# A decoder layer on one core: GpSimd takes three eighths of attention's products for the first two tiles

## The chip, the cores and the metric

The kernel runs on one core of a Trainium2 chip. The metric is the device time of one execution in microseconds. Three runs of the kernel before gave 707.16, 707.42 and 708.32 us; their median, 707.42 us, is the time before.

## The reference, cut to what matters

A decoder layer with its normalisations behind each part (float32, x of shape 2 x 512 x 1024):

```python
x = layernorm(x + attn(x))            # attention within a token, over the D = 32 channels of 32 heads
x = layernorm(x + xattn(x, ctx))      # fake_quant(x) @ fake_quant(ctx)
x = layernorm(x + ffn(x))             # relu(x@up)**2 @ down + x@fc1@expert@fc2 * routing, normalised

# attn, for each token: q, k, v are [D, H] each; k and v have 8 heads, repeated 4 times
scores = einsum('bsdh,bseh->bsde', q, k) / sqrt(D)
out    = einsum('bsde,bseh->bsdh', softmax(scores), v)
```

The attention mixes the 32 x 32 channel pairs of each token, and no tokens. There is one such small product per token, so it is done elementwise: the tokens lie on the 128 partitions, and the products and sums run along the free dimension.

## The kernel before, in words

The 1024 tokens are eight tiles of 128, t = 0 to 7, and two tiles (`TB = 2`) are a block. The heads that share a k and v are summed first, so each token has q, k and v of 32 x 8 values.

**Front.** TensorE projects tiles 0 and 1 (`project_qk` L153, `project_v` L158) as the weights arrive. Then `fill()` gives it work while the first two tiles go through attention: projections of tiles 2 to 7, then transposes of an expert matrix (L425) and a product of weights (L447). For each tile of `fill()`, x is loaded (`xs`), transposed by TensorE (L134, `pt_x`) and copied from PSUM by ScalarE in two halves (L135, `xT`); the transposes of the next tile stand behind the fifth of the current tile's eight steps. The results are copied by ScalarE (L185, L186) and added by GpSimd's DMAs to biases that lie in DRAM (L191, L192, `qkv_d`); `fetch_qkv` (L175, L176) brings them back when their tile is due. Between these, ScalarE turns the eight tiles of the first context into codes, in three passes each (L364, L367, L370); a context tile's load waits on SyncE's queue for one of the room that earlier ones leave.

**A tile's tokens.** `token_path()` walks through the tiles. `scores(t)` makes q times k in four quarters c (`DC = 8` rows of the 32): a product of 2048 elements for each partition (L463) into `prod`, of which there are two buffers, then a sum over the 8 heads (L469). Both are VectorE's. `exponentials` takes the maximum, subtracts it (L479, on VectorE), and has ScalarE do the exponentials (L482). `attend` sums these (`den`, L488), and makes four more quarters with v: product (L496), sum (L502). Then it multiplies by the reciprocal of `den` (L507) and adds x. For tile 0 that addition (L517) also gives the sum for the mean, and `normalise_aside` does the rest of the normalisation on ScalarE (L335, L340, L342, L348, L349), with an inverse root by GpSimd (L344); tile 1 is normalised on VectorE (`normalise`, L325, its root at L319). `cross` quantises the tile (on ScalarE for tile 0, from L364 on; on VectorE for tile 1, L353 to L355), transposes the codes (`pta`) and multiplies by the context's codes on TensorE (`py`, L654), and normalises again. The sums of the context's codes (`pc`, L580) come in between.

**The feed-forward part.** Block 0 begins when both its tiles are through, at about 144 us of the trace. From then on TensorE works at the feed-forward products (L816, L1046, and for the last two blocks together L931 and L1306), and the attention of tiles 2 to 7 goes on beside it on VectorE. Tile 2's first products stand behind the second normalisation of tile 1 (`last`).

**What sets the order.** The engines run their own queues in order. A planner fixes these when the kernel is built: it takes the instructions as the Python program emits them, with its own costs for each, and may move an instruction ahead of others. `tc.issue_after(x)` pins an instruction behind x on the queue. How far the token path is ahead of the filling work is set by the weights that the generators yield.

Of the kernel before, what the change touches and what calls it, by code (L numbers as in the profile page):

```python
# [12 lines left out]
ALU = mybir.AluOpType  # L13
# [3 lines left out]
P = 128  # L17
# [10 lines left out]
def kernel(  # L28
# [24 lines left out]
    nc = tc.nc  # L53

    B, S, E = x.shape
    _, D, H = wq.shape
    G = wk.shape[2]
# [11 lines left out]
    TB = 2  # L69
# [3 lines left out]
    DC = 8  # L73
# [248 lines left out]
    def normalise(t, name):  # L322

        mean, rstd = mean_rstd([t[:, ts(h, HALF)] for h in range(E // HALF)], name)
        return nc.vector.tensor_scalar(t, t, mean, rstd, ALU.subtract, ALU.mult)  # L325

    def normalise_aside(t, sums, name):

        n = sums.shape[-1]
        parts = small.tile([P, 2], F32, tag="parts", name=f"parts_{name}")  # L330
        minus = parts[:, 0:1]
        if n > 1:
            minus = small.tile([P, 1], F32, tag="minus", name=f"minus_{name}")
        with behind_acted(True):
            nc.scalar.activation(  # L335
                parts[:, 0:n], sums, AF.Copy, scale=-1.0 / E, accum_out=minus if n > 1 else None
            )
        square = attp.tile([P, E], BF16, tag="square", name=f"square_{name}")
        total = small.tile([P, 1], F32, tag="square", name=f"squares_{name}")
        nc.scalar.activation(square, t, AF.Square, bias=minus, accum_out=total)  # L340
        ve = small.tile([P, 1], F32, tag="ve", name=f"ve_{name}")
        nc.scalar.activation(ve, total, AF.Identity, scale=1.0 / E, bias=eps)  # L342
        rstd = small.tile([P, 1], F32, tag="rstd", name=f"rstd_{name}")
        nc.gpsimd.tensor_tensor(rstd, ve, neg_half, ALU.pow)  # L344
        yield 3.0
        shift = small.tile([P, 1], F32, tag="shift", name=f"shift_{name}")
        with behind_acted(True):
            nc.scalar.activation(shift, rstd, AF.Identity, scale=minus)  # L348
        return nc.scalar.activation(t, t, AF.Identity, scale=rstd, bias=shift)  # L349
# [103 lines left out]
            nc.gpsimd.dma_start(e2[ts(l, P), :], row)  # L453


    def scores(t, qk, behind=None):
        q3 = qk[:, 0:DG].rearrange("p (d g) -> p d g", g=G)
        k3 = qk[:, DG : 2 * DG].rearrange("p (e g) -> p e g", g=G)
        s = tokp.tile([P, D, D], F32, tag="s", name=f"s_{t}", bufs=2)
        for c in range(D // DC):  # L460
            prod = tokp.tile([P, DC * D * G], F32, tag="prod", name=f"pqk_{t}_{c}", bufs=2)
            with tc.issue_after(behind.ins) if behind is not None else ExitStack():
                nc.vector.tensor_tensor(  # L463
                    prod.rearrange("p (d e g) -> p d e g", d=DC, g=G),
                    q3[:, ts(c, DC), :].unsqueeze(2).to_broadcast([P, DC, D, G]),
                    k3.unsqueeze(1).to_broadcast([P, DC, D, G]),
                    ALU.mult,
                )
            nc.vector.tensor_reduce(  # L469
                s[:, ts(c, DC), :].rearrange("p d e -> p (d e)"),  # L470
                prod.rearrange("p (c g) -> p c g", g=G), AX.X, ALU.add,
            )
            yield 4.6
        return s
# [11 lines left out]
    def attend(t, xc, s, v):  # L486
        den = small.tile([P, D], F32, tag="den", name=f"den_{t}")
        nc.vector.tensor_reduce(den, s, AX.X, ALU.add)  # L488
        rden = small.tile([P, D], F32, tag="rden", name=f"rden_{t}")
        nc.vector.reciprocal(rden, den)  # L490
        yield 2.0

        o = tokp.tile([P, D, G], F32, tag="o", name=f"o_{t}")
        for c in range(D // DC):
            prod = tokp.tile([P, DC * D * G], F32, tag="prod", name=f"pav_{t}_{c}", bufs=2)
            nc.vector.tensor_tensor(  # L496
                prod.rearrange("p (d g e) -> p d g e", d=DC, g=G),
                s[:, ts(c, DC), :].unsqueeze(2).to_broadcast([P, DC, G, D]),
                v.unsqueeze(1).to_broadcast([P, DC, G, D]),
                ALU.mult,  # L500
            )
            nc.vector.tensor_reduce(  # L502
                o[:, ts(c, DC), :].rearrange("p d g -> p (d g)"),
                prod.rearrange("p (c e) -> p c e", e=D), AX.X, ALU.add,
            )
            yield 4.6
        nc.vector.tensor_tensor(o, o, rden.unsqueeze(2).to_broadcast([P, D, G]), ALU.mult)  # L507

        x3 = xc.rearrange("p (c j) -> p c j", j=J)
        o3 = o.rearrange("p d g -> p (d g)").unsqueeze(2).to_broadcast([P, DG, J])  # L510
        if t == TB - 1:

            nc.vector.tensor_tensor(x3, x3, o3, ALU.add)
            normalise(xc, f"1_{t}")
        else:
            sums = small.tile([P, 1], F32, tag="sum1", name=f"sum1_{t}")
            nc.vector.scalar_tensor_tensor(x3, x3, 1.0, o3, ALU.mult, ALU.add, accum_out=sums)  # L517
            yield 1.0
            yield from normalise_aside(xc, sums, f"1_{t}")
        yield 3.0  # L520
# [151 lines left out]
    def token_path():  # L672
# [5 lines left out]
        def begin(t):  # L678
            xc = xpool.tile([P, E], F32, tag="xc", name=f"xc_{t}")
            nc.sync.dma_start(xc, xf[ts(t, P), :])  # L680
            qk, v = qkv.pop(t)
            if 0 < t < NT - 1:
                fetch_qkv(t + 1)
            at[t] = xc, v, scores(t, qk, last if t == TB else None)
# [13 lines left out]
        for blk in range(NBLK):  # L698
            xcs = []
            x2T = []  # L700
            for i in range(TB):
# [4 lines left out]
                if t == 0:  # L706

                    begin(1)
                    yield next(at[1][2])
                yield from attend(t, xc, done[t], v)  # L710
                if t % (S // P) == 0:
                    b = t // (S // P)
# [763 lines left out]
```

## Time and profile before

| | |
|---|---|
| median of three runs | 707.42 us |
| the profiled execution: its time, and its span from first to last instruction | 707.94 us, 706.2 us |
| granted TensorE clock | 0.991 |
| VectorE products q x k (L463), 32 of them | 72.4 us, 2282 ns each |
| VectorE sums over heads (L469), 32 | 72.3 us, 2277 ns each |
| VectorE products with v (L496), 32 | 72.5 us, 2281 ns each |
| VectorE sums over channels (L502), 32 | 72.0 us, 2265 ns each |
| GpSimd inverse roots (L344), 21 | 21.2 us, 1008 ns each |
| front, 32 to 90 us: busy TensorE, VectorE, ScalarE, GpSimd | 57.70, 54.97, 45.40, 9.62 us |

Busy times are sums over the instructions of an engine in one profiled execution; the mean of one is its own duration, and consecutive independent instructions on VectorE overlap by some 0.08 us, so that a product of 2282 ns comes every 2.20 us. Idle time of an engine costs something only where another waits for it. PE is TensorE's matmuls, DVE VectorE, ACT ScalarE, POOL GpSimd, SP SyncE. L12 is line 12 of the kernel before.

### The profile page before, as it was taken

The page shows a single profiled execution, that of the slowest core. Times are in us where ns is not written, and L with a number is a line of the kernel's source. Part 1 is how long each engine was busy: PE and PEld are TensorE (multiplying, and loading weights), DVE is VectorE, ACT ScalarE, POOL GpSimd, SP SyncE. Part 2 cuts the span into 40 slices and gives each one's busy share as a digit, 9 for nine tenths or more (in the row PEclk, how much of TensorE's full clock was granted, in tenths as well). Part 3 has the DMA queues.
Part 4 walks back from the last instruction along what each step waited for, and adds up shares of the span by engine and source line. Part 5 has one row for each costly group of instructions (what it writes and reads, how often), then busy time and mean ns, then how long its engine had stood idle before and what let it go on. Part 6 is the DMA issues. An engine that isn't in the chain of part 4 may idle for free.

```text
span 706.2 us, 7444 instructions
## 1 busy us (share of the span) xinstructions
PE 682.7 (97%) x2798; PEld 482.6 (68%) x2808; DVE 586.4 (83%) x678; ACT 262.1 (37%) x440; POOL 76.6 (11%) x107
## 2 busy tenths in 40 slices
PE   8999999999999999998999999999999999999991
PEld 3666654578876444477876444478888888888881
DVE  5799987699999999699999960297787688897895
ACT  1297643322636458517626233122251200000252
POOL 1011212200010122001002000020110000001012
PEclk9999999999999999999999999999999999999997
DMA  9989729485446548345536433667997445567733
GB/s 339 304 264 366 204 25 295 104 298 162 144 134 167 184 177 267 136 159 190 173 120 167 176 121 132 233 184 242 355 331 264 153 175 163 171 198 190 208 85 119
DMA packets 70900, 139.08 MB, mean 197 GB/s; under 512 B 5264, under 2 KB 39696, under 8 KB 70864
## 3 DMA queue, kind: packets, MB, share of 16 engines
q1 hardware_dynamic: 60656, 106.87, 44.6%
q0 software_dynamic: 10064, 31.47, 16.1%
q8 instruction: 22, 0.36, 0.2%
q10 hardware_dynamic: 144, 0.26, 0.1%
q14 instruction: 14, 0.11, 0.0%
HBM read 114.99 MB, written 21.50 MB: 193 GB/s over the span
## 4 chain that ended last, share of the span: by engine, by line
PE 40%; issue 6%; DVE 4%; ACT 3%; DMA 2%; POOL 1%; POOLq 0%; DVEq 0%; ACTq 0%
PE pd L1046 9%; PE pp L931 9%; PE ps L1306 5%; PE pp_mm L931 5%; PE pp_tr L931 4%; PE ps_mm L1306 2%; PE ps_tr L1306 2%; PE pu L816 2%; DMA dn<-tw 1%; ACT square L340 1%; PE py L654 1%; DMA y_a<-xc 1%; POOL rstd L344 1%; DVE pav L496 1%; PE pl L816 1%
## 5 line engine op out<-in xcount | busy, mean ns | idle before, releaser
L1046 PE MATMUL pd<-dn,h 128*128 128x512 f32 x320 | 139.3, 593 | 0.0
L816 PE MATMUL pu<-x2T,up 128*128 128x256 f32 x512 | 113.4, 380 | 2.3 <-ACT relu L832 2.3
L1046 PEld LDWEIGHTS pd<-dn,h 128*128 128x128 f32 x320 | 60.3, 190 | 71.8 <-issue 71.3
L816 PEld LDWEIGHTS pu<-x2T,up 128*128 128x128 f32 x512 | 96.4, 190 | 16.9 <-ACT relu L832 3.2
L496 DVE TENSOR_TENSOR pav<-s,v 128x2048 f32<-128x2048 f32 x32 | 72.5, 2281 | 0.0
L463 DVE TENSOR_TENSOR pqk<-qk 128x2048 f32<-128x2048 f32 x32 | 72.4, 2282 | 0.0
L469 DVE TENSOR_REDUCE s<-pqk 128x256 f32<-128x2048 f32 x32 | 72.3, 2277 | 0.1
L502 DVE TENSOR_REDUCE o<-pav 128x64 f32<-128x2048 f32 x32 | 72.0, 2265 | 0.0
L153 PE MATMUL pqk<-wqkv,xT 128*128 128x512 f32 x128 | 65.1, 609 | 1.9 <-DVE wqkv L244 1.6
L158 PEld LDWEIGHTS pv<-wqkv,xT 128*128 128x128 f32 x128 | 24.3, 190 | 24.2 <-issue 22.7
L344 POOL TENSOR_TENSOR rstd<-ve,neg_half 128x1 f32<-128x1 f32 x21 | 21.2, 1008 | 174.5 <-ACT ve L342 171.2
L158 PE MATMUL pv<-wqkv,xT 128*128 128x256 f32 x128 | 35.6, 379 | 0.0
L659 DVE SCALAR_TENSOR_TENSOR xc<-py,ns,xc 128x512 f32<-128x512 f32 x16 | 11.7, 742 | 26.5 <-PE py L654 26.5
L153 PEld LDWEIGHTS pqk<-wqkv,xT 128*128 128x128 f32 x128 | 24.3, 195 | 13.3 <-issue 7.3
L832 ACT ACTIVATE relu<-pu 128x256 f32<-128x256 f32 x32 | 12.1, 377 | 51.5 <-PE pu L816 51.5
L1210 DVE TENSOR_TENSOR tt<-dn 128x1024 f32<-128x1024 f32 (+1 forms) x20 | 21.2, 1059 | 10.8 <-DMA dn<-in_L_ffn_down_w_dram 6.4
L654 PE MATMUL py<-cq,aT 128*128 128x512 bf16 x120 | 27.5, 379 | 1.5 <-ACT aT L642 1.1
L816 PE MATMUL pl<-x2T,fc 128*128 128x256 f32 x128 | 28.2, 380 | 0.5 <-ACT latent L845 0.5
L447 PE MATMUL pe<-fc,exT 128*128 128x512 f32 x64 | 28.7, 594 | 0.0
L816 PEld LDWEIGHTS pl<-x2T,fc 128*128 128x128 f32 x128 | 24.2, 190 | 4.3 <-ACT latent L845 0.9
L654 PEld LDWEIGHTS <-aT 128*128 128x128 bf16 x128 | 12.4, 98 | 17.0 <-issue 2.0
L642 ACT COPY aT<-pta 128x1024 bf16<-128x1024 bf16 x7 | 7.0, 1007 | 43.9 <-PE pta L641 43.9
(311 smaller groups left out, 1163.1 us busy)
## 6 DMA issues: line engine op xcount, KB each, us to landing
up<-in_L_ffn_up_w_dram SPq DMA_DIRECT2D x16, 1024.0 KB, 5.5
dn<-in_L_ffn_down_w_dram SPq DMA_DIRECT2D x16, 1024.0 KB, 4.9
pair<-in_L_ffn_up_w_dram SPq DMA_DIRECT2D x8, 1024.0 KB, 6.3
dn<-tw SPq DMA_DIRECT2D x8, 1024.0 KB, 5.0
tw<-outer POOLq DMA_DIRECT2D x7, 1024.0 KB, 5.3
fc<-in_L_ffn_fc_w_dram SPq DMA_DIRECT2D x6, 1024.0 KB, 5.6
dn<-in_L_ffn_down_w_dram SPq DMA_DIRECT2D x12, 512.0 KB, 5.5
outer<-in_L_ffn_down_w_dram SPq DMA_DIRECT2D x5, 1024.0 KB, 5.1
```

The costliest lines, as they stand in the source:

```text
L153: projecting[0] = nc.tensor.matmul(pqk, xT[:, k, :], wqkv[k][:, 0 : 2 * DG], start=(k == 0), stop=(k == KE - 1))
L158: nc.tensor.matmul(pv[:, :DG], xT[:, k, :], wqkv[k][:, 2 * DG : 3 * DG], start=(k == 0), stop=(k == KE - 1),)
L447: expert[0] = nc.tensor.matmul(ps, exT[m // 2][:, m % 2, ts(l, P)], fc2[m // 2][:, m % 2, ts(n, HALF)], start=(m == 0), stop=(m == NL - 1),)
L463: nc.vector.tensor_tensor(prod.rearrange("p (d e g) -> p d e g", d=DC, g=G), q3[:, ts(c, DC), :].unsqueeze(2).to_broadcast([P, DC, D, G]), ...
L469: nc.vector.tensor_reduce(s[:, ts(c, DC), :].rearrange("p d e -> p (d e)"), prod.rearrange("p (c g) -> p c g", g=G), AX.X, ALU.add,)
L496: nc.vector.tensor_tensor(prod.rearrange("p (d g e) -> p d g e", d=DC, g=G), s[:, ts(c, DC), :].unsqueeze(2).to_broadcast([P, DC, G, D]), ...
L502: nc.vector.tensor_reduce(o[:, ts(c, DC), :].rearrange("p d g -> p (d g)"), prod.rearrange("p (c e) -> p c e", e=D), AX.X, ALU.add,)
L654: crossed[t] = nc.tensor.matmul(py, aT[:, k, :], cq[:, k, ts(h, HALF)], start=(k == 0), stop=(k == KC - 1))
L816: lately[0] = nc.tensor.matmul(ps[:, :NB], ws[:, k, wcols], xT[:, k, :], start=(k == 0), stop=(k == KE - 1))
L931: lately[0] = nc.tensor.matmul(banks[m], steps[g][m][:, k, :], moving[m][:, k, :], start=(k == 0 and m not in (6, 3, 7)), stop=(k == KH - ...
L1046: lately[0] = nc.tensor.matmul(pd[i][n], h[:, kk // 4, i, kk % 4, :], w[:, k, ts(n, HALF)], start=(kk == 0), stop=(kk == NK - 1),)
L1306: lately[0] = nc.tensor.matmul(banks[mm], unit(o, mm, j), inner_weights[o, cc][mm][:, j - lo, :], start=(j == 0 and mm not in FIRST_OF), s ...
```

## The change

For tiles 0 and 1 (`t < TB`) each product of a quarter is split along its eight rows: VectorE makes the first five (1280 elements), GpSimd the last three (768, `ASIDE = 3`), both into the same `prod`. VectorE's sum of the quarter then needs both. VectorE's part is pinned behind the latest sum that was emitted (`added_up`), so on VectorE's queue product and sum alternate; GpSimd's part has no such pin. That holds for both kinds of products, q x k and with v: 16 products in all. Tiles 2 to 7 keep their products whole on VectorE.

```diff
+    ASIDE = 3
+    added_up = [None]
+
+    def shares(t, behind=None):
+
+        pin = ExitStack()
+        for before in (behind, added_up[0] if t < TB else None):
+            if before is not None:
+                pin.enter_context(tc.issue_after(before.ins))
+        if t < TB:
+            yield nc.vector, 0, DC - ASIDE, pin
+            yield nc.gpsimd, DC - ASIDE, DC, ExitStack()
+        else:
+            yield nc.vector, 0, DC, pin
+
     def scores(t, qk, behind=None):
...
             prod = tokp.tile([P, DC * D * G], F32, tag="prod", name=f"pqk_{t}_{c}", bufs=2)
-            with tc.issue_after(behind.ins) if behind is not None else ExitStack():
-                nc.vector.tensor_tensor(
-                    prod.rearrange("p (d e g) -> p d e g", d=DC, g=G),
-                    q3[:, ts(c, DC), :].unsqueeze(2).to_broadcast([P, DC, D, G]),
-                    k3.unsqueeze(1).to_broadcast([P, DC, D, G]),
-                    ALU.mult,
-                )
-            nc.vector.tensor_reduce(
+            for engine, lo, hi, pin in shares(t, behind):
+                with pin:
+                    engine.tensor_tensor(
+                        prod.rearrange("p (d e g) -> p d e g", d=DC, g=G)[:, lo:hi],
+                        q3[:, c * DC + lo : c * DC + hi, :].unsqueeze(2).to_broadcast(
+                            [P, hi - lo, D, G]
+                        ),
+                        k3.unsqueeze(1).to_broadcast([P, hi - lo, D, G]),
+                        ALU.mult,
+                    )
+            added_up[0] = nc.vector.tensor_reduce(
                 s[:, ts(c, DC), :].rearrange("p d e -> p (d e)"),
                 prod.rearrange("p (c g) -> p c g", g=G), AX.X, ALU.add,
             )
...
         for c in range(D // DC):
             prod = tokp.tile([P, DC * D * G], F32, tag="prod", name=f"pav_{t}_{c}", bufs=2)
-            nc.vector.tensor_tensor(
...
-            nc.vector.tensor_reduce(
+            for engine, lo, hi, pin in shares(t):
...
+            added_up[0] = nc.vector.tensor_reduce(
```

The planner lays out the queues anew. TensorE's and SyncE's instructions keep their order in the whole kernel. On VectorE, product and sum alternate for tiles 0 and 1, and the bias additions to `v` (L694) stand between a product and a sum. On ScalarE the exponentials of tile 0 move ahead of a code pass (L370), and tile 0's first normalisation moves forward: its square, variance, shift, scaling and first quantising pass now stand ahead of the two copies of tile 6's `xT`. GpSimd's queue has the 16 new products between its DMAs and its roots.

More of the change, by code (lines that the diff above doesn't have):

```diff
@@ L495, in attend @@
             prod = tokp.tile([P, DC * D * G], F32, tag="prod", name=f"pav_{t}_{c}", bufs=2)
[L496 to L502, printed above, removed]
+            for engine, lo, hi, pin in shares(t):
+                with pin:
+                    engine.tensor_tensor(
+                        prod.rearrange("p (d g e) -> p d g e", d=DC, g=G)[:, lo:hi],
+                        s[:, c * DC + lo : c * DC + hi, :].unsqueeze(2).to_broadcast(
+                            [P, hi - lo, G, D]
+                        ),
+                        v.unsqueeze(1).to_broadcast([P, hi - lo, G, D]),
+                        ALU.mult,
+                    )
+            added_up[0] = nc.vector.tensor_reduce(
                 o[:, ts(c, DC), :].rearrange("p d g -> p (d g)"),
```

## The prediction

> **What bounds the kernel now.** I read the engine table of the page first, then the busy time by stretches, TensorE's waits, and the instructions in order of time on ScalarE, TensorE, GpSimd and VectorE.
>
> ```profile
> PE 682.7 (97%) x2798; PEld 482.6 (68%) x2808; DVE 586.4 (83%) x678; ACT 262.1 (37%) x440; POOL 76.6 (11%) x107
> ```
>
> The page's engine table: TensorE is busy for 97% of 706.2 us. In the stretch that the change touches it is fuller still (stretch; busy us of PE, PEld, DVE, ACT, POOL; clock; DMA share; GB/s):
>
> ```profile
> 32.00:90.00 58.00, 57.70 (x212) 35.56 (x211) 54.97 (x34) 45.40 (x57) 9.62 (x12) 1.00 0.86 277
> ```
>
> TensorE idles for 0.3 of 58 us, VectorE for 3. Both look full, but only TensorE sets the end: its waits from 20 to 145 us are three, for 0.9 us together:
>
> ```profile
> PE pt_ex L425 <- ACT exT L426: 0.3, 1, 0.3
> PE pqk L153 <- ACT xT L135: 0.3, 1, 0.3
> PE pta L619 <- DVE a L355: 0.3, 1, 0.3
> ```
>
> So no more than 0.9 us can be won there, whatever VectorE does. The third wait, the one on VectorE, stays: GpSimd makes tile 1's root (120.23) behind tile 0's (119.67), and that one follows tile 0's `py` products, whose place in TensorE's queue is fixed (113.46). Tile 2's attention is pinned behind tile 1's second normalisation, which follows TensorE's `py` of tile 1 (128.34). VectorE, finished sooner with tiles 0 and 1, waits for TensorE.
>
> The question is what can hold TensorE up. Its instruction order is the same in the changed kernel, and so is SyncE's. ScalarE's is not. In before, the two copies of tile 6's transposed x stand ahead of tile 0's normalisation:
>
> ```profile
> 71.68 1.15 ACT L367 ACTIVATE ctx<-ctx,round_up 128x1024 f32<-128x1024 f32 x1
> 72.86 1.15 ACT L370 ACTIVATE cq<-ctx,top_down 128x1024 bf16<-128x1024 f32 x1
> 74.50 1.07 ACT L135 COPY xT<-pt_x 128x512 f32<-128x512 f32 x2 [0.49 <-PE pt_x L134]
> 78.67 0.20 ACT L335 ACTIVATE parts<-sum 128x1 f32<-128x1 f32 x1 [3.09 <-DVE xc L517]
> 78.90 1.15 ACT L340 ACTIVATE square<-xc,parts 128x1024 bf16<-128x1024 f32 x1
> ...
> 83.49 0.30 ACT L348 ACTIVATE shift<-rstd,parts 128x1 f32<-128x1 f32 x1 [2.30 <-POOL rstd L344]
> 83.82 1.25 ACT L349 ACTIVATE xc<-xc,shift,rstd 128x1024 f32<-128x1024 f32 x1
> 85.10 1.24 ACT L364 ACTIVATE qt<-xc,z,rs 128x1024 f32<-128x1024 f32 x1
> ```
> ```profile
> 73.87 1.04 PE L134 MATMUL pt_x<-ident,xs 128*128 128x128 f32 x8
> ...
> 78.61 1.02 PE L153 MATMUL pqk<-wqkv,xT 128*128 128x512 f32 x2
> ```
>
> (Start, us, engine, line, operation.) TensorE transposes tile 6 at 73.87, still has tile 5's last three steps to do, and needs the first copy at 78.61; it was there at 75.0. In the changed kernel ScalarE's order is: sum scaled (L335), last code pass (L370), square, variance, shift, normalise (L349), first quantising pass (L364), and only then these copies. They now depend on VectorE's sum of tile 0 (L517) and on GpSimd's root.
>
> **Part by part.** *VectorE's products.* 16 products shrink from 2048 to 1280 elements. Products follow one another at 2.20 us (32.38 and 34.58), some 0.07 of it fixed: 2.13 x 1280/2048 + 0.07 = 1.40. That saves 0.80 each, 12.8 in all. Ahead of tile 0's sum stand 10 products in place of 11: 10 x 0.80 + 2.20 = 10.2 us earlier, before any new wait.
>
> *GpSimd's products*, 16 of 768 elements; no such row exists. Rows: a memset of 128 elements took 0.205 us, an affine select of 128 took 0.32, a memset of one 0.10. Bounds: the memset less its fixed part, 0.8 ns an element, 0.7 us; the select's 2.5 ns plus the 0.56 of a one-element root, 2.5 us. Between the gross rates of memset (1.6 ns) and select (2.5 ns) lie 1.23 and 1.92; their middle plus 0.1 is **1.7 us**, which I take: a product streams elements as these two do, and has no root to find.
>
> *Turns between GpSimd and VectorE.* Here the trace is telling. GpSimd's root, a one-element operation with two inputs, took 0.57 us at 119.67, when VectorE was idle, but:
>
> ```profile
> 260.51 1.84 POOL L344 TENSOR_TENSOR rstd<-ve,neg_half 128x1 f32<-128x1 f32 x1 [0.77 <-ACT ve L342]
> ```
> ```profile
> 259.65 2.28 DVE L496 TENSOR_TENSOR pav<-s,v 128x2048 f32<-128x2048 f32 x1
> 261.85 2.28 DVE L463 TENSOR_TENSOR pqk<-qk 128x2048 f32<-128x2048 f32 x1
> 264.05 2.28 DVE L502 TENSOR_REDUCE o<-pav 128x64 f32<-128x2048 f32 x1
> ```
>
> It ended at 262.35, 0.42 after VectorE's product ended at 261.93. The same holds at 82.02 (ended 83.46, product 83.03), 229.38 and 277.46. Beside a reduction (339.82) it took 0.56. So GpSimd's two-input operations wait for VectorE's, not for its sums; and at 261.93 GpSimd, which had asked first, came in ahead of a second product. I read this as turns, given to whoever asked first; a GpSimd product of 1.7 us would then hold up the next two-input VectorE operation. The row itself bounds that hold from below at nothing (the product at 261.85 still took 2.28, behind one element), and from above at the whole 1.7. [...] I take the whole, since a held element shows the order of turns and cannot show their length.
>
> Product and sum alternate on VectorE, so mostly GpSimd's next product can run beside the sum (1.7 against 2.20) and nothing is lost. But four times, before tile 0's sum, a small two-input operation stands between them while GpSimd waits for its turn: `s12d2` (L288) after the second product, the bias additions to `v` (L694) after the third and fourth, `o` x `rden` (L507). Each then waits about 1.75 us: **7.0**. Further: GpSimd's first product starts only after VectorE's first, so the first sum waits 1.2; before the first `pav` product GpSimd's, released by the same exponentials while VectorE still sums `den`, is in front by 0.7; VectorE's wait for the exponentials (0.79) grows by 0.4; small operations and orders that changed about 0.9. Sum 10.2: the whole saving. Tile 0's sum stays at about **78.6**.
>
> *ScalarE's queue.* From there, by the rows above: L335 0.15, L370 1.03, square with its accumulator 1.25, variance 0.32, root 0.65 (0.08 to be seen, 0.57), shift 0.34, L349 to L364 1.31, L364 to a following independent one 1.13 (36.39 to 37.52), first copy 0.57, TensorE 0.05: 6.8. So TensorE gets its copy at 85.4 instead of having been able to start at 78.61: **+6.8 us**. The earlier reordering, tile 0's exponentials ahead of a code pass and of tile 4's copies, makes those ready near 56.2, just when TensorE wants them (56.22); nothing there, or a few tenths that the later wait contains.
>
> *GpSimd's queue.* Its products stand in front of and behind the DMAs that add projections to `qkv_d` and fetch them (L191, L192, L175, L176). The fetched tiles are first used at 135 us, so some us of delay are covered by 50; if that cover went, tile 2 would wait for all of it. The product of tile 1's last quarter stands ahead of tile 0's root, in the same window as the 6.8; it ends before the root's input comes.
>
> *What follows* moves as a whole: from 85 us TensorE has 0.6 us of wait until 145, tile 2 hangs on TensorE, and no wait is there to absorb 6.8. VectorE's 12.8 saved us win nothing.
>
> Against the profiled execution (span 706.2, 707.94 in all): 707.94 + 6.8 = 714.7. The median of its runs is 0.5 lower: **714.2 us**.
>
> **The rivals.** (a) VectorE is not held: it keeps its turn, or GpSimd's product does not shut it out. Then only the start (1.2), the exponentials (0.6), `pav`'s first product behind GpSimd's fetch at 50.76 (1.6) and about 0.6 of small things are lost: tile 0's sum comes at 72.4 or earlier. ScalarE is not free before 72.72, because the last context tile lands at 67.60; L370 starts at 72.86, and the chain ends at 79.5. TensorE waits 0.9: 707.4 + 0.9 = **708.3**, no change within what can be measured, 0.2% or 1.4 us. It decides wherever tile 0's sum comes before 72.7. If the context tile also landed 0.9 earlier, nothing would be left: 707.4. For it: no VectorE product in the trace was ever seen delayed. Against it: the root at 260.51.
>
> (b) GpSimd is dearer (2.5 us), or gets ahead of VectorE's own products as well. At 2.5 the products no longer fit beside a sum, each waiting operation loses 0.8 more and each of the quarters some 0.3: 4 x 0.8 + 8 x 0.3 = 5.6, hence +12.4: **719.8**. For it: four dimensions with repeated operands, which no row shows.
>
> (c) A gain. TensorE's 0.9 us of waits in the window are all there is to win, under the 1.4 us that can be told from no change: at best **706.5**.
>
> **How the numbers follow.** Forecast 0.57 (at 0.7 to 2.2 us a product it gives +1.4 to +10), (a) 0.25, (b) 0.15, (c) a gain 0.03. Slower by over 0.2%: 0.57 + 0.15 + 0.05 from (a) with a dearer product = 0.77; same 0.20; faster 0.03. Range: from the middle of (a), 708.2, to near (b), 718.5; it leaves out about 0.1 on each side. The forecast's own range is 710 to 717.5.
>
> **What would show it.** In the profile after: GpSimd products of about 1.7 us, each ending well after a VectorE product beside it; `v` additions (0.41 before) or `o` x `rden` stretched or late by about 1.7; tile 0's sum near 78.6 (72.4 in (a)); TensorE with a wait of about 6.8 at `pqk` on ScalarE's `xT`, near 78.6, and the same rows as before behind it. I am wrong if that wait is under 1.4, if TensorE waits elsewhere (`pc`, `pta`), or if a VectorE product itself is held.

## The result and the profile after

The changed kernel takes 715.57 us (median of four executions, 713.13 to 716.28) against 707.29 for the kernel before on the same chip: a ratio of 1.0109, with a 95% interval of 1.0092 to 1.0126. It is slower by about 8 us; 714.2 was predicted. The profiled execution took 716.28 us, with a span of 714.5 (before: 707.94 and 706.2).

The engine table first:

```profile
PE 686.6 (96%) x2808; PEld 483.9 (68%) x2808; DVE 586.1 (82%) x678; ACT 262.2 (37%) x440; POOL 118.0 (17%) x123
```

VectorE gave 16 x 0.8 = 12.8 us of products away and is as busy as before (586.4). GpSimd has 41 us more, nearly all of it 16 products whose rows are 2.85 (q x k) and 2.48 us (with v) long on average. A row's length on either engine includes the time in which the instruction has been issued but cannot run yet, so these numbers show the waiting as well as the work: the product at 34.55 has a row of 3.12 us, of which 1.66 are its own time (below). The stretch that the change touches (us; busy us of PE, PEld, DVE, ACT, POOL; clock; DMA share; GB/s):

```profile
32.00:90.00 58.00, 51.90 (x176) 31.60 (x177) 56.29 (x35) 43.33 (x54) 32.08 (x22) 0.94 0.83 276
```

TensorE lost 5.8 of the 57.7 us that it worked there, and its clock fell from 1.00 to 0.94. Its waits between 20 and 146 us (engine, line, waited for; us in total, times, longest):

```profile
PE pqk L153 <- ACT xT L135: 5.0, 2, 4.7
PE pt_x L134 <- DMA xs<-in_x_dram: 1.7, 1, 1.7
PE pt_ex L425 <- ACT exT L426: 0.3, 1, 0.3
PE pta L641 <- DVE a L355: 0.2, 1, 0.2
```

The first is the one that was predicted. The second, on the loaded tile 2 of x near 31 us, is also in the profiles of kernels that take 707 us (the order alone, below), so it is no effect of the change. In order of time, the row that carries the wait and its neighbours:

```profile
76.23 1.04 PE L134 MATMUL pt_x<-ident,xs 128*128 128x128 f32 x8
...
85.82 2.08 PE L153 MATMUL pqk<-wqkv,xT 128*128 128x512 f32 x2 [4.68 <-ACT xT L135]
87.69 1.06 PE L158 MATMUL pv<-wqkv,xT 128*128 128x256 f32 x2
88.54 1.23 PE L153 MATMUL pqk<-wqkv,xT 128*128 128x512 f32 x2
90.05 1.02 PE L153 MATMUL pqk<-wqkv,xT 128*128 128x512 f32 x2
```

The second step of tile 6's projection in before:

```profile
79.90 1.02 PE L153 MATMUL pqk<-wqkv,xT 128*128 128x512 f32 x2
```

TensorE begins tile 6's projection at 85.82 in place of 78.61: +7.2 us. Of these only 4.68 are seen as a wait, for in this profile TensorE was behind already: it transposes tile 6 at 76.23, not 73.87. Of these 2.4 us, 0.75 go back to the loads near 31 and 1.6 to two steps at half speed behind them (34.48 to 38.77). A TensorE that had been on time would have waited so much longer for the same copy. Its products then come back at half speed: two of 512 take 2.08 us, not 1.02. One step of the projection is 1.29 us long (78.61 to 79.90 in before); the first two here take 2.72 and 1.51, which is 1.65 us more. Together 8.85; the next fixed point, `pc`, stands at 98.66 against 89.81, 8.85 later, and `pg`, the start of the gate products, at 152.56 against 143.72, 8.84 later. Between these points nothing is given back or added; at the end of the span 8.3 of it are left.

Why the copies come late is on ScalarE:

```profile
79.03 0.20 ACT L335 ACTIVATE parts<-sum 128x1 f32<-128x1 f32 x1 [4.02 <-DVE xc L539]
79.14 1.13 ACT L370 ACTIVATE cq<-ctx,top_down 128x1024 bf16<-128x1024 f32 x1
...
82.46 0.29 ACT L348 ACTIVATE shift<-rstd,parts 128x1 f32<-128x1 f32 x1 [0.73 <-POOL rstd L344]
82.79 1.24 ACT L349 ACTIVATE xc<-xc,shift,rstd 128x1024 f32<-128x1024 f32 x1
84.06 1.24 ACT L364 ACTIVATE qt<-xc,z,rs 128x1024 f32<-128x1024 f32 x1
85.21 1.05 ACT L135 COPY xT<-pt_x 128x512 f32<-128x512 f32 x2
```

ScalarE idles for 4.02 us on VectorE's sum of tile 0, though tile 6's x is transposed by 77.3, and copies it only at 85.21. And why the sum is not earlier is on VectorE and GpSimd:

```profile
34.53 1.48 DVE L479 TENSOR_TENSOR pqk<-qk 128x1280 f32<-128x1280 f32 x1
35.93 2.02 DVE L716 TENSOR_TENSOR v<-v,bv_ge 128x256 f32<-128x256 f32 x1
...
53.80 4.75 DVE L516 TENSOR_TENSOR pav<-s,v 128x1280 f32<-128x1280 f32 x1
...
73.64 2.03 DVE L529 TENSOR_TENSOR o<-o,rden 128x256 f32<-128x256 f32 x1
...
77.78 1.21 DVE L539 SCALAR_TENSOR_TENSOR xc<-xc,o 128x1024 f32<-128x1024 f32 x1
```
```profile
34.55 3.12 POOL L479 TENSOR_TENSOR pqk<-qk 128x768 f32<-128x768 f32 x1 [2.29 <-DVE s L487]
...
53.60 3.60 POOL L516 TENSOR_TENSOR pav<-s,v 128x768 f32<-128x768 f32 x2
```

The same two small operations in before:

```profile
41.17 0.41 DVE L694 TENSOR_TENSOR v<-v,bv_ge 128x256 f32<-128x256 f32 x1
...
74.87 0.42 DVE L507 TENSOR_TENSOR o<-o,rden 128x256 f32<-128x256 f32 x1
```

Two products start together at 34.5: VectorE's is that of the third quarter, GpSimd's already that of the fourth. VectorE's ends at 36.01, GpSimd's at 37.67: 1.66 us later, its own time. The addition to `v`, 0.41 us in before, is issued at 35.93 and ends at 37.95, right behind GpSimd's product. `o` x `rden` does the same (0.42 to 2.03).

### The profile page after: what moved, and what is told of

The parts are those of the page before. It is cut to its first block, busy times and chain, and to the rows that moved or that the text cites. A ratio compares the mean times of both kernels' runs of the same rounds, so it can differ in the third digit from the quotient of the medians.

```text
span 714.5 us, 7484 instructions
## 1 busy us (share of the span) xinstructions
PE 686.6 (96%) x2808; PEld 483.9 (68%) x2808; DVE 586.1 (82%) x678; ACT 262.2 (37%) x440; POOL 118.0 (17%) x123
## 4 chain that ended last, share of the span: by engine, by line
PE 43%; issue 5%; ACT 3%; DVE 2%; POOL 1%; POOLq 0%
PE pd L1068 9%; PE pp L953 8%; PE ps L1328 7%; PE pp_mm L953 5%; PE ps_mm L1328 4%; PE pp_tr L953 4%; PE ps_tr L1328 3%; PE pu L838 1%; ACT square L340 1%; PE py L676 1%; POOL rstd L344 1%; DVE pav L516 1%; PE pl L838 1%; PE pt_x L134 0%; ACT xc L349 0%
## 5 line engine op out<-in xcount | busy, mean ns | idle before, releaser
L487 DVE TENSOR_REDUCE s<-pqk 128x256 f32<-128x2048 f32 x32 | 72.4, 2279 | 1.3 <-POOL pqk L479 1.0
L516 DVE TENSOR_TENSOR pav<-s,v 128x2048 f32<-128x2048 f32 (+1 forms) x32 | 70.1, 2202 | 0.0
L479 DVE TENSOR_TENSOR pqk<-qk 128x2048 f32<-128x2048 f32 (+1 forms) x32 | 67.7, 2133 | 0.0
L479 POOL TENSOR_TENSOR pqk<-qk 128x768 f32<-128x768 f32 x8 | 22.8, 2854 | 21.3 <-DVE qk L183 13.9
```

Source lines behind the costliest of these rows:

```text
L479: engine.tensor_tensor(prod.rearrange("p (d e g) -> p d e g", d=DC, g=G)[:, lo:hi], q3[:, c * DC + lo : c * DC + hi, :].unsqueeze(2).to_br ...
L487: added_up[0] = nc.vector.tensor_reduce(s[:, ts(c, DC), :].rearrange("p d e -> p (d e)"), prod.rearrange("p (c g) -> p c g", g=G), AX.X, A ...
L516: engine.tensor_tensor(prod.rearrange("p (d g e) -> p d g e", d=DC, g=G)[:, lo:hi], s[:, c * DC + lo : c * DC + hi, :].unsqueeze(2).to_bro ...
```

## The experiments

The theory was: VectorE's saving is eaten because its small two-input operations wait for GpSimd's products; ScalarE's new order then passes the late sum on to TensorE. The main rivals: the order alone costs, GpSimd's load costs in some other way, or the loss is somewhere else. All ratios are to the kernel before, run beside each kernel; they are those of the record and differ from the quotient of the two medians by up to 0.12%. Sum 0 is the end of tile 0's sum; `pg` is the start of the gate products, against 143.72 in before, in the profiled execution. VectorE's first product begins at 22.9 to 26.3 us in these profiles, so the column behind sum 0 counts from there.

| kernel | median us (before beside it) | ratio, 95% interval | sum 0, us | from VectorE's first product, us | wait for tile 6's xT, us | `pg` later by |
|---|---|---|---|---|---|---|
| before | | | 78.63 | 54.0 | 0 | 0 |
| after | 715.57 (707.29) | 1.0109 (1.0092 to 1.0126) | 78.99 | 55.5 | 4.7 | 8.8 |
| after, again | 714.70 (706.91) | 1.0101 (1.0080 to 1.0123) | 78.82 | 55.4 | 4.7 | 8.7 |
| e9, memsets | 708.68 (707.14) | 1.0030 (1.0012 to 1.0048) | 71.25 | 48.0 | 1.0 | 1.8 |
| e10, copies | 708.22 (707.17) | 1.0021 (1.0000 to 1.0043) | 71.80 | 48.6 | 1.8 | 2.4 |
| e6, one eighth | 706.92 (707.17) | 0.9997 (0.9984 to 1.0011) | 77.82 | 52.9 | 0.8 | 1.4 |
| e7, fewer held | 710.94 (707.14) | 1.0060 (1.0036 to 1.0084) | 74.96 | 51.2 | 2.1 | 3.3 |
| e2, order only | 706.95 (707.17) | 0.9993 (0.9982 to 1.0003) | 76.58 | 53.0 | 0 | 0.8 |
| e3, split only | 715.75 (706.91) | 1.0119 (1.0097 to 1.0141) | 83.64 | 57.3 | 7.8 | 11.3 |
| e1, copies ahead | 710.36 (707.14) | 1.0034 (1.0017 to 1.0052) | 75.98 | 52.8 | 0 | 1.1 |
| e11, root ahead too | 707.78 (707.17) | 0.9998 (0.9984 to 1.0013) | 75.74 | 52.8 | 0 | 0.1 |
| e8, kept awake | 711.92 (707.14) | 1.0063 (1.0046 to 1.0080) | 77.83 | 52.8 | 1.2 | 6.2 |
| e12, one turn | 714.81 (706.91) | 1.0105 (1.0080 to 1.0130) | 76.55 | 52.8 | 3.6 | 7.6 |

Executions of one kernel differ by 2 to 9 us (e2 by 2.0, e7 by 7.9, e10 by 8.8), so the columns behind the ratio, which are from one of them, and the median need not agree closer than that.

**What is it that holds VectorE?** First, GpSimd's instructions in their places, without their reading (`prod_part`, and `operand_part` below, stand for the slices):

```diff
+                    if engine is nc.gpsimd:
+                        engine.memset(prod_part, 1.0)
+                        continue
```

> GpSimd's 16 products are replaced by memsets of the same 768 elements (the attention of tiles 0 and 1 is wrong for three eighths); orders as in the changed kernel. Theory (VectorE's two-input operations are shut out by GpSimd's reading): the v additions are back at 0.41 us, s12d2 at 0.14, tile 0's sum at 72 or earlier, TensorE waits 1 us or less: 708.5 to 710. Rival (any GpSimd instruction that uses SBUF shuts VectorE out, writes too): holds as long as GpSimd's instruction, 712 to 716.

It took 708.68 us. VectorE's rows are short again, and a product of 1.47 us runs beside a GpSimd memset of 0.74, neither of them held:

```profile
33.14 0.42 DVE L722 TENSOR_TENSOR v<-v,bv_ge 128x256 f32<-128x256 f32 x1
...
54.74 1.47 DVE L522 TENSOR_TENSOR pav<-s,v 128x1280 f32<-128x1280 f32 x1
```
```profile
54.88 0.74 POOL L520 MEMSET pav<- 128x768 f32 x1 [2.53 <-DVE o L530]
```

With no holds the sum comes at 71.25 and TensorE waits 1.0: the prediction's rival (a), with its numbers (72.4 or earlier, 0.9). But a memset is also shorter than a product and reads nothing. So next GpSimd reads one operand:

```diff
+                    if engine is nc.gpsimd:
+                        engine.tensor_copy(prod_part, operand_part)
+                        continue
```

> GpSimd's products are replaced by copies of one operand of the same shape (768 elements), so its instructions stay with their places and semaphores but read one input instead of two; the products' last three eighths are wrong in value. VectorE and the orders are those of after. Two theories. Held by any GpSimd instruction that reads SBUF: VectorE's two-input operations still wait for the whole copy (0.8 to 1.6 us by its duration), tile 0's sum comes at 74 to 78 and the time is 710 to 714. Held only by a GpSimd instruction with two inputs: v additions 0.42, o x rden 0.42, products 1.48, tile 0's sum near 71.3, time 708.3 to 709.5 as in e9_memset.

```profile
32.22 1.48 DVE L482 TENSOR_TENSOR pqk<-qk 128x1280 f32<-128x1280 f32 x1
33.63 1.04 DVE L722 TENSOR_TENSOR v<-v,bv_ge 128x256 f32<-128x256 f32 x1
```
```profile
32.23 2.16 POOL L480 COPY pqk<-qk 128x768 f32<-128x768 f32 x1 [2.27 <-DVE s L490]
```

The copy ends at 34.39, 0.69 after VectorE's product: its own time, shorter than I had thought. The addition to `v` takes 0.62 more than alone. So an instruction with one input holds VectorE as one with two does, for as long as it lasts. The sum (71.80) and the time (708.22) fell below what that theory gave, because 0.69 us fits nearly everywhere; only the rows tell the two theories apart here, the time does not.

Third, a product of another size (`ASIDE = 3` becomes 1, 256 elements):

> GpSimd makes one eighth of each product (256 elements) in place of three eighths. Nothing is left out. If a hold lasts as long as GpSimd's product: that product takes about 0.62 us (0.1 fixed + a third of 1.56), each held operation loses about 0.5, in all some 5 us against the 4.9 saved (10 x 0.27 + 2.2), so tile 0's sum is at 77 to 79. ScalarE's copies of tile 6 stand behind the sum scaled, a code pass and the square only, 2.5 us behind the sum, so TensorE waits about 2 to 3 us: 709 to 711.5. If a turn has a fixed price (1.6 us whatever the size): held operations still take 1.6 to 2.0, the sum comes near 82 and the time is 713 or more. If holds vanish with so small a product: sum near 74, no wait, 707.2.

```profile
37.33 0.95 DVE L716 TENSOR_TENSOR v<-v,bv_ge 128x256 f32<-128x256 f32 x1
```
```profile
35.48 2.51 POOL L479 TENSOR_TENSOR pqk<-qk 128x256 f32<-128x256 f32 x1 [2.36 <-DVE s L487]
```

GpSimd's product ends 0.58 us after VectorE's (37.99 and 37.41), and the addition is held by 0.53. The sum came at 77.82, in the expected range. The time did not: 706.92, no difference, where 709 to 711.5 was expected. In this order the last code pass was done before the sum came, so ScalarE reached the copies 1.4 us behind it (79.25), not 2.5 to 3, and TensorE waited 0.8.

Three GpSimd instructions that read, of 0.58, 0.69 and 1.66 us, hold the addition by 0.53, 0.62 and 1.61: the hold is the instruction's own time less 0.05 to 0.07. A memset of 0.74 does not: the product beside it takes 1.47 us. At each change of turns in these rows GpSimd, already waiting, goes ahead of VectorE's next two-input operation (in after it is issued at 34.55, the addition at 35.93).

**Which held operations cost?** Take three of the small ones away:

```diff
-        nc.vector.tensor_mul(s12d2, s12, d2)
+        nc.scalar.activation(s12d2, s12, AF.Copy, scale=d2)
...
-            if t < TB:
-                v = at[t][1]
-                nc.vector.tensor_add(v, v, bv_ge)
```

> The changed kernel without three of the small two-input VectorE operations that were held: the two additions of the bias to v are left out (so tiles 0 and 1 lack the bias of v), and s12d2 is made by ScalarE. ScalarE's order stays as in the changed kernel. Theory (those holds make tile 0's sum late, 1.55 + 2 x 1.95 us): the sum comes about 5 us earlier, near 73.5, ScalarE is then bound by its own code passes to 75, TensorE's wait shrinks from 4.7 to about 0.7 and the slow products go: 709 to 711 us. Rival (the sum is late for another reason, GpSimd's rate or its queue): 714 to 716.

The median, 710.94 us, is in the expected range, but three of ten executions took 714 to 716.3, and the sum (74.96 for about 73.5) and the wait (2.1 for 0.7) came later than expected. Nor is all of the gain due to the small operations: in this profile GpSimd's first `pav` product came behind VectorE's, which was not held (1.48), and the sum behind it waited 1.45 instead. The hold of `s12d2` did not go, it passed to the next two-input operation:

```profile
30.82 1.70 DVE L290 SCALAR_TENSOR_TENSOR kd2s12d<-d,s12d 128x1 f32<-128x1 f32 x1
```

So it is the place that costs, behind a product while GpSimd's waits, and not the operation.

**Order or split?** The change has two parts. The order alone (VectorE makes whole products, pinned as in after):

```diff
-        if t < TB:
-            yield nc.vector, 0, DC - ASIDE, pin
-            yield nc.gpsimd, DC - ASIDE, DC, ExitStack()
-        else:
-            yield nc.vector, 0, DC, pin
+        yield nc.vector, 0, DC, pin
```

> The order without the split: VectorE makes whole products of 2048 elements for all tiles, and those of tiles 0 and 1 stand behind the sum of the quarter ahead; GpSimd makes none. Nothing is left out. My theory: order alone moves tile 0's sum by about one product (78.6 to near 76.4 or 78), ScalarE's order is that of before, with tile 6's copies ahead of tile 0's normalisation, so nothing reaches TensorE: 706.8 to 707.8, as before. Rival: the order itself costs (each product now starts behind a sum, and what was interleaved is lost): over 708.5.

706.95: no difference. The sum comes 2.0 us earlier. One of these is an earlier start of VectorE, the other is left of the one product less that stands ahead of it. ScalarE keeps the order of before, and nobody uses the gain. The split alone:

```diff
-        for before in (behind, added_up[0] if t < TB else None):
+        for before in (behind, None):
```

> The split without the order: GpSimd makes three eighths as in the changed kernel, but VectorE's products don't wait for the sum of the quarter ahead, so two of them follow one another. Nothing is left out. ScalarE's copies of tile 6 then stand behind tile 0's normalisation but ahead of the first quantising pass (1.15 us less than in the changed kernel). My theory of turns: GpSimd's product, asked for while VectorE's runs, comes next, so now the second of two VectorE products is held by 1.6 us where the additions to v are not; and 11 products stand ahead of tile 0's sum in place of 10 (1.4 us more). Sum at 77.5 to 81, copies 5.6 us behind it, TensorE waits 4.5 to 8 us and then runs slowly for 1 to 2: 712 to 717, with some VectorE products of about 3 us in the profile. Rival: VectorE's own products never lose a turn (they were 1.48 long almost everywhere in the changed kernel because its order shields them for another reason): no product is long, the sum is at 75 to 77, and the time 708 to 711.

715.75 us: as slow as both parts together. Without the order VectorE's own products lose turns, while the additions to `v`, now behind a sum, take 0.41 again:

```profile
69.06 1.47 DVE L516 TENSOR_TENSOR pav<-s,v 128x1280 f32<-128x1280 f32 x1
70.45 3.10 DVE L479 TENSOR_TENSOR pqk<-qk 128x1280 f32<-128x1280 f32 x1
...
78.19 4.32 DVE L479 TENSOR_TENSOR pqk<-qk 128x1280 f32<-128x1280 f32 x1
```

The second of two adjacent products takes 3.10, that is 1.62 more; the last one, 4.32, stands ahead of tile 0's sum. Its 2.84 are more than one GpSimd product; GpSimd issues two DMAs in that time as well, and what share is theirs no run shows. The sum ends at 83.64, 2.6 us past the end of what I expected, but VectorE also began 2.8 us later than in after; counted from its first product the sum is 1.9 us later than in after. So the split loses, and the order only shields VectorE's products from part of it.

**Is it ScalarE's order that reaches TensorE?** Tile 0's first normalising step and tile 1's exponentials pinned behind tile 6's copies, VectorE and GpSimd as in after:

```diff
-        with behind_acted(True):
+        with tc.issue_after(turned[0].ins) if name == "1_0" else behind_acted(True):
...
+        with tc.issue_after(turned[0].ins) if t == TB - 1 else ExitStack():
```

> The split stays; only ScalarE's order is put back: tile 0's first normalisation stands behind tile 6's two copies of xT, tile 1's exponentials behind tile 7's. Theory (TensorE loses its time only at those copies): the wait of 4.7 us goes, and with it the slow products behind it; 707.3 to 708.7 us, no different from before by 0.2%, with VectorE's operations held by GpSimd as long as in the changed kernel. Rival (GpSimd's products cost by themselves, through VectorE's chain or the DMAs in GpSimd's queue): 712 or more.

TensorE's wait of 4.7 is gone with the holds in place (`o` x `rden` 2.04, sum at 75.98). But the median is 710.36, with executions from 707.0 to 713.0 where 707.3 to 708.7 was expected; the miss was a second wait that I had not looked for. In the profile, which caught the fastest execution (707.02), ScalarE waits 5.12 us for GpSimd's root, and GpSimd for a DMA:

```profile
84.59 0.29 ACT L348 ACTIVATE shift<-rstd,parts 128x1 f32<-128x1 f32 x1 [5.12 <-POOL rstd L344]
```
```profile
83.33 0.61 POOL L175 DMA_DIRECT2D qk<-qkv_d  x1 [5.69 <-issue]
83.96 0.59 POOL L344 TENSOR_TENSOR rstd<-ve,neg_half 128x1 f32<-128x1 f32 x1
```

In this order GpSimd's fetch of tile 3, which needs the addition into `qkv_d`, stands ahead of the root, and the copies of projections out of PSUM stand behind the shift on ScalarE. So one more pin, for that fetch:

```diff
+        with tc.issue_after(roots["1_0"].ins) if t == TB + 1 else ExitStack():
             nc.gpsimd.dma_start(qk, qkv_d[t, :, 0 : 2 * DG])
```

> The kernel of e1_copies_first with one more order: GpSimd's fetch of tile 3's projection (it waits for the addition into qkv_d) is issued behind tile 0's root, not ahead of it. Nothing of the computation is left out. My theory: in e1 the executions of 710 to 713 us come from that fetch, which kept the root back by 5 us in the profile; ScalarE then copies a projection out of PSUM late and TensorE waits at the next one. Then this kernel takes 706.8 to 707.8 in all its executions, ScalarE waits under 1 us for the root, TensorE has no wait over 0.5 between 60 and 100 us, and tile 0's sum still comes at 77 to 79 with VectorE's holds as they were. Rival: the spread comes from the start (loads, clock) or from GpSimd's products themselves; then the median stays near 710 and the spread stays.

```profile
79.35 0.29 ACT L351 ACTIVATE shift<-rstd,parts 128x1 f32<-128x1 f32 x1 [0.67 <-POOL rstd L346]
```

707.78 us, no difference from before, with executions (706.1 to 709.9) spread as those of before beside them (705.6 to 709.7), though not all within the 706.8 to 707.8 that I expected. So with GpSimd's products and the holds of the four small operations kept, changed orders on ScalarE and GpSimd alone give back the whole loss. It is no gain either: the sum comes 2.9 us earlier than in before (1.7 of it from an earlier start), and nobody uses that.

**The slow products behind the wait.** 18 products into an unused bank fill TensorE's wait:

```diff
+            if t == NT - 2:
+                with tc.issue_after(projecting[0].ins):
+                    keep_awake(18)
```

> The changed kernel with 18 small products of ones put into TensorE's queue ahead of tile 6's first product, to fill the wait (3.9 us at full rate). Theory (after the idle time TensorE's products run at half rate for 2.7 us and cost 1.6 more): behind the wait products are 0.43 us apart at once, 1.2 to 1.8 us faster than the changed kernel, about 714. Rival (the slow products are not due to the idle time): as the changed kernel, 715.6.

```profile
79.41 4.05 PE L228 MATMUL awake<-onesb 128*128 128x512 bf16 x18
84.66 1.13 PE L153 MATMUL pqk<-wqkv,xT 128*128 128x512 f32 x2 [1.20 <-ACT xT L135]
86.05 1.02 PE L153 MATMUL pqk<-wqkv,xT 128*128 128x512 f32 x2
```

The steps behind the copy are 1.39 and 1.29 us long at once, and the time is 711.92, 3.7 below the changed kernel where 1.2 to 1.8 was expected. Part of the surplus is that in this profile the sum came at 77.83, not 78.99, although VectorE began 1.5 us later: the first `pav` product was held behind one GpSimd product (2.08 us), not two (4.75). Products of half speed follow waits of 4.68, 3.64 and 7.8 us (after, e12, e3) for 3.1 to 5.5 us, and waits of 1.0 to 2.1 at this place not at all, as if only the length of the wait counted. The wait near 31 us (1.71, and 0.30 behind the transposes) doesn't fit that: in both profiles of after products of half speed followed it, in seven other profiles with the same wait they did not. The granted clock, read from the traces in steps of 0.2 us, shows more. In after it is 0.50 from 34.35 to 37.76 and from 85.55 to 88.96, in e12 from 82.1 to 88.9, in e3 from 84.6 to 91.4: 3.4 us each time or twice that. The changes in after, with its last fall at 703.4, lie 1, 14, 1 and 180 times 3.413 us apart. In the trace of after, then, the clock changes only on a grid of 3.41 us. That the cost of a wait depends also on where it falls on the grid is my estimate from these five changes; no run here moves a wait on purpose to show it, and why the short wait near 31 sufficed in two profiles stays open.

**One GpSimd product or two?** That difference was tried in two ways: the changed kernel once more, and one in which GpSimd's second `pav` product must wait for VectorE's first.

```diff
+                if t < TB and c == 1 and engine is nc.gpsimd:
+                    pin.enter_context(tc.issue_after(first[0].ins))
...
+                if t < TB and c == 0 and engine is nc.vector:
+                    first = [made]
```

> The changed kernel once more, nothing altered, to see how far its executions differ among themselves. In its first profile VectorE's first product of attend was held behind two of GpSimd's (4.75 us); in the profiles of three kernels with the same order on VectorE and GpSimd (e1, e8, e11) it was held behind one (2.08). My theory: which of the two happens is decided anew in each execution, by whether GpSimd's fetch of tile 2 ends just before or after VectorE asks; the two differ by 2.7 us in tile 0's sum and by as much in TensorE's wait. Then the times lie in a group near 713 and one near 716, and a profile with 2.08 shows the sum near 76.5, a wait of 2 to 2.5 us and little or no slow products. Rival: 4.75 belongs to this kernel; then all times lie at 715 to 716.5 and the profile shows it again.

> The changed kernel with one semaphore more for tiles 0 and 1: GpSimd's second product of attend also waits for VectorE's first one, so that it can't take a second turn ahead of it. The order on each engine is that of the changed kernel and nothing is left out. My theory: the first product takes 2.1 us in each execution, tile 0's sum comes 2.7 us earlier than in the changed kernel's first profile (near 76.3), TensorE's wait at tile 6's projection is 2 to 2.5 us in place of 4.7 and its products behind it run at the full rate: 711 to 713.2. Rival: the double turn costs nothing because the later holds absorb it: 715 to 716.

Both missed. The second profile of after has the double turn again (4.68 us), and its six executions (712.0 to 716.5) show no two groups. e12 has 2.08 in its profile, the sum at 76.55 and TensorE's first product at 83.41, 2.25 us earlier than in after, but the time is 714.81, that of after beside it. Half of the 2.25 went to slow products:

```profile
83.41 2.07 PE L153 MATMUL pqk<-wqkv,xT 128*128 128x512 f32 x2 [3.64 <-ACT xT L135]
85.27 1.06 PE L158 MATMUL pv<-wqkv,xT 128*128 128x256 f32 x2
86.13 1.92 PE L153 MATMUL pqk<-wqkv,xT 128*128 128x512 f32 x2
```

Its first three steps take 2.72, 2.56 and 1.40 us, 2.81 over three of 1.29, against 1.65 in after: the clock came back near 88.9 in both. In the profile 1.2 us remain (`pg` +7.6, not +8.8); in the medians nothing can be seen. Counted from VectorE's first product, the sum comes after 52.8 us in all four profiles with the single turn (e1, e8, e11, e12) and after 55.4 to 55.5 in both of after, so the double turn costs the sum 2.6 us. It goes with GpSimd's first product beginning 0.2 to 0.83 us ahead of VectorE's (after, after again, e3), the single one with 1.08. How often it happens in after, and why e12, which rules it out, is no faster in its median, stays open. That the clock came back at the same time in both profiles takes away half of the gain, but not all of it.

No kernel here beats the one before: e2, e6 and e11 are at its time, their intervals within 0.2% on either side. In before TensorE waits for nothing at tile 6's projection, so there is nothing there that an earlier sum could win.

## Why the prediction was right, and where it was off

- **Where it is lost.** TensorE at `pqk` of tile 6, waiting for ScalarE's `xT`: as predicted. Tile 0's sum was to come at 78.6; it came at 78.99. The copy was to reach TensorE at 85.4; it did at 85.82. +6.8 was predicted for this term, +7.2 measured. The chain on ScalarE from the sum to TensorE, added up to 6.8 from ten rows, took 6.83. The wait that is seen was 4.68 and not 6.8, since TensorE came to it late. e1 shows that ScalarE's order carries most of the loss, e11 that with GpSimd's fetch behind the root nothing is left of it.
- **GpSimd's price**, taken between two bounds as 1.7 us: 1.66. That it is so close is luck: it is the middle between the rates of a memset and a select, and a memset of the same size took 0.74.
- **The holds.** Four of 1.75 were predicted, from a turn that one row had shown; no row of before shows the length, a whole product, which was an estimate. Measured: 1.55 (`s12d2`), 1.61 twice (`v`), 1.61 (`o` x `rden`), 6.4 in all for 7.0. That the hold is the whole product, which a one-element root couldn't show, is now shown by three lengths.
- **The first `pav` product** was mis-sized: 0.7 for half a product ahead of it, measured 3.27, since two products came ahead. In the profiles with a single turn it is 0.6, close to what was predicted. The first sum's wait was 0.97 for 1.2; the exponentials' wait was 1.12, 0.33 more than in before, for 0.4. The sum is met as closely as it is because VectorE's part began 1.05 us earlier in the profiled execution (23.54 against 24.59), which is luck; without that it would have been at 80, and the term 1.4 too small. With a single turn it would have been 1.2 too large.
- **The step that was missing**: TensorE did not come back from its wait of 4.68 us at full speed. 1.65 us, a fifth of the loss. The prediction put nothing for it. It moved later work "as a whole", and up to `pg` it does move as a whole, but 8.84 us and not 6.8. By the profile this is the larger part of what the forecast lacks.
- **Rivals.** (a), VectorE not held, is what e9 measured: its sum, its wait of 1.0 and its time (708.3 predicted, 708.68 measured) stand; only the condition failed. Of (b), GpSimd ahead of VectorE's own products was seen, in e3 and in the first `pav` product. (c), a gain, could only come from TensorE's waits in before, 0.9 us in all, and no kernel here is faster than before.
- **Said to be wrong if** a VectorE product itself is held: three were, one ahead of tile 0's sum (4.75 us) and two behind it (3.08 at 78.92 and 2.07 at 92.95). The first changed a term, not the path.

## What to carry to other kernels

Before work goes from VectorE to GpSimd, list each two-input VectorE operation that will stand between the shared products: here each lost nearly a whole GpSimd instruction (1.55 to 1.61 us for one of 1.66), however small it was itself, and taking one away could hand its hold to the next (a row of 1.70 us for `kd2s12d` in e7, 0.15 in after); a fill that reads nothing held nothing (1.47 us for the product beside a memset of 0.74). Then ask who uses the time that is won: here TensorE set the end, so the most that could come back was below 1 us, while the planner's new order put some six microseconds of normalisation ahead of the copies that TensorE needs. (Why it chose so, no run shows.) When a wait of some microseconds comes to TensorE, count a slow start behind it as well: here 1.65 us behind 4.68, 2.81 behind 3.64.

## What the runs showed that was not expected

- A GpSimd copy with one input takes 0.69 us for 768 elements, a product 1.66, and both hold VectorE's two-input operations for nearly their whole length (0.62 and 1.61); a memset of the same size, 0.74, does not (1.47 for the product beside it).
- GpSimd's own time goes with the elements: 0.58 us for 256, 1.66 for 768, 2.1 ns for each element more.
- GpSimd can take two turns in a row ahead of a waiting VectorE product (4.75 us for 1.48 of work), where its second product is queued directly behind the first.
- VectorE's reductions are not touched: 2.27 to 2.29 us beside a GpSimd product, as alone (2.28 in before).
- In after TensorE's granted clock fell and came back only on a grid of 3.41 us (34.35, 37.76, 85.55, 88.96 and 703.4). A wait of 4.68 us was followed by 1.65 us of loss (after), a shorter one of 3.64 us by 2.81 (e12).
